# Opening order of the loads: three pieces of the input projection first, A_log and the attention constants behind the convolutions

## The chip, the cores and the metric

The kernel runs on one core of a Trainium2 chip. The metric is device time in microseconds (us) of one launch, from which the median of several runs is taken. A core has a matrix engine (TensorE, in the views PE, and PEld for its weight loads), VectorE (DVE), ScalarE (ACT), GpSimd (POOL) and SyncE (SP). In this kernel SP does nothing but issue DMAs; its rows in the timeline, marked SPq, show the time that each issue took on the queue, not the transfer. [...]

## What is computed

The reference is one decoder layer on x of shape (8, 512, 512) in float32, with a layer norm after each of three parts:

```
x = layernorm(x + mamba(x))                 # ln, in_proj, causal conv (4 taps), silu, x_proj, dt, scan, gate, out_proj
x = layernorm(x + cross_attention(x, ctx))  # 16 heads of 32
x = layernorm(x + mixture_of_experts(x))    # 32 experts, 4 for each token, plus a shared one
```

The change touches the start of the first part. There, for each sequence, `xz = xn @ in_proj_w` gives x_main and z (1024 columns each), x_main goes through a convolution of four taps along time and a silu, `x_dbl = x_main @ x_proj_w` gives dt, B and C, and the scan is `h = exp(A dt) * h + dt B x`, with `A = -exp(A_log)` of shape (1024, 16).

## The kernel before

**Chunks.** The function `layers` cuts the 8 sequences of 512 steps into 16 chunks of 256 steps. Inside a chunk 32 steps run over four pairs of channel blocks (q), four groups of states (g) and the two blocks of a pair: `decays` (L437, ACT) makes exp(A dt), `scan` multiplies (L449) and scans (L453) on DVE, and `collect` multiplies by C (L470, DVE) and sums over states on PE (L474). Attention and routing of the sequence before are placed between the steps. The function `experts` runs the 32 experts after that, and `finish` the last layer norm.

**The start.** Ahead of the first step stand: the load of the first chunk of x (L168), its layer norm (L74 to L80), the transposes (L286) and their scaling by ln_w and ln_b (L291), four convolutions, `silu` (L353), `x_proj` (L359) with its result stored to DRAM (L367), `prepare` (dt and dt x, L389 to L412) with the copies `both` (L418), and the broadcasts `bc` (L378) of B and C. A convolution (`convolve`) is a projection on PE (L302, 16 matmuls with one piece of in_proj_w), a copy out of PSUM on ACT (L322), the first tap on ACT (L328) and six instructions for the other taps on DVE (L336). Buffer `xp`, which L322 writes, is there once, so a convolution's copy waits for the taps of the one before.

**The pieces of weights.** `pieces()` is a generator over the 512 KB pieces of in_proj_w and out_proj_w in the order of their use; three buffers named `wm` hold them. Each piece is loaded by SP (L156). `begun` draws the first piece at once. The generator loads one piece ahead of the one that it hands out: the start loads pieces 0 and 1, the second convolution asks for piece 2 while it takes piece 1, the third asks for piece 3, the fourth for piece 4, which is the first of z.

**The constants.** After `begun(pieces())` the source loads nine small constants with `const` (L131: ln_w to res_scale), then A_log in 16 DMAs of 4 KB (L185, into `aneg`), then bq, bk, bv, bo and wg (L131). Further down, behind memsets on POOL, six DMAs (L241) put rows of ones into the three attention buffers `ka`, and one DMA writes zeros to the DRAM tensor `based` (L258). The first use of `aneg` is an exponential on ACT (L1032) and a negation on DVE (L1033); both are in place, ahead of the first `decays`. bq, bv and bo are used in `biases` (L974, L986, L990), which also takes the attention mask (L976 to L980).

**What sets the order.** The source order is a wish. The tile framework's planner puts the instructions of each engine in an order of its own, by the source order as a priority and by its own estimate of when inputs and buffers are there; only `silu` is pinned. That is why in the trace before the weights Wo (L525), the mask (L976) and the next chunk of x (L271), which stand inside the first chunk's steps in the source, are issued at 29 to 31 us, and why some of the 32 DMAs that fill the experts' input buffer with zeros (`clear`, L262, 1362.5 KB each), also placed inside the first two chunks, are issued before the first scan. Within `layers` the calls stand in this order:

```
    for q in range(CC // 2):
        do(convolve, 0, q, f, first=(q == 0))
    dry()
    silu(*f["xs"].values())
    do(x_proj, f)
    dry()
    do(prepare, 0, f)
    dry()
    bc, n = bcast(f, 0), 0
```

Of the kernel before, what the change touches and what calls it, by code (L numbers as in the profile page):

```python
# [8 lines left out]
F32 = mybir.dt.float32  # L9
# [8 lines left out]
P = 128  # L18
B, S, D = 8, 512, 512
DC = D // P  # L20
# [4 lines left out]
NST = 16  # L25
# [4 lines left out]
NG = 4  # L30
HP = P // 2
NPB = 3

NH = 16
HD = 32
SC = S // P

E = 32
# [44 lines left out]
def layers(ctx, tc, a, x1d, filld, based, xbuf):  # L83
# [23 lines left out]
    nc = tc.nc  # L107
# [3 lines left out]
    cp = ctx.enter_context(tc.tile_pool(name="l_const", bufs=1))  # L111
# [17 lines left out]
    def const(name, shape, src):  # L129
        t = cp.tile(shape, F32, name=f"l_{name}")  # L130
        nc.sync.dma_start(t, src)  # L131
        return t

    def rows(w):
        return w.rearrange("(c p) f -> p c f", p=P)

    def pieces():


        w_in, w_out = rows(a["in_proj_w"]), rows(a["out_proj_w"])  # L140
        xs = [w_in[:, :, 2 * q * P : 2 * (q + 1) * P] for q in range(CC // 2)]
        zs = [w_in[:, :, DI + 2 * q * P : DI + 2 * (q + 1) * P] for q in range(CC // 2)]
        outs = [w_out[:, 2 * q : 2 * q + 2, :] for q in range(CC // 2)]
        n = B * (S // T)
        order = list(xs)
        for i in range(n):
            order += (outs if i else []) + zs + (xs if i + 1 < n else [])
        order += outs
        got = None
        for src in order + [None]:  # L150
            nxt = None
            if src is not None:
                nxt = mp.tile([P, 4 * 2 * P], F32, tag="wm", name="wm", bufs=3).rearrange(
                    "p (c f) -> p c f", c=src.shape[1]
                )
                nc.sync.dma_start(nxt, src)  # L156
            if got is not None:
                yield got
            got = nxt

    def begun(it):
        first = next(it)
# [4 lines left out]
    x0 = p1.tile([P, NT_, D], F32, tag="xt", name="xt")  # L167
    nc.sync.dma_start(x0, a["x"][0, 0:T, :].rearrange("(j p) d -> p j d", p=P))  # L168
    piece = begun(pieces())
    lnw = const("lnw", [P, DC], a["ln_w"])  # L170
    lnb = const("lnb", [P, DC], a["ln_b"])
# [4 lines left out]
    b_dt = const("b_dt", [P, CC], a["dt_proj_b"])  # L176
    dpar = const("dpar", [P, CC], a["D_param"])
    rs = const("rs", [P, 1], a["res_scale"].partition_broadcast(P))

    aneg = cp.tile([P, CC, 2, NST // NG, NG // 2], F32, name="l_aneg")  # L180
    for r in range(2):
        for j in range(2):
            for g in range(NST // NG):
                n0 = g * NG + r * NG // 2
                nc.sync.dma_start(  # L185
                    aneg[r * HP : (r + 1) * HP, :, j, g, :],
                    rows(a["A_log"])[j * HP : (j + 1) * HP, :, n0 : n0 + NG // 2],
                )
    bq = const("bq", [P, DC], a["bq"])
    bk = const("bk", [P, DC], a["bk"])  # L190
    bv = const("bv", [P, DC], a["bv"].rearrange("(c p) -> p c", p=P))
    bo = const("bo", [P, D], a["bo"].partition_broadcast(P))
    wg = const("wg", [P, DC, E], rows(a["wg"]))

    conv_tail = cp.tile([P, CC, 3], F32, name="l_conv_tail")
# [8 lines left out]
    ones = cp.tile([P, P], F32, name="l_ones")  # L206
# [26 lines left out]
    qas, kas = [], []  # L233
    for i in range(NPB):
        qas.append(cp.tile([P, S], F32, name=f"l_qa{i}"))
        kas.append(cp.tile([P, S], F32, name=f"l_ka{i}"))
        for t in (qas[i], kas[i]):
            for r0 in (HD, 2 * HD + HD):
                nc.gpsimd.memset(t[r0 : r0 + HD], 1.0 if t is qas[i] else 0.0)
        for r0 in (HD + 1, 2 * HD + HD + 1):  # L240
            nc.sync.dma_start(  # L241
                kas[i][r0 : r0 + 1, :].rearrange("p (c t) -> p c t", c=DC),
                ones[0:1, :].unsqueeze(1).to_broadcast([1, DC, P]),
            )
    va = cp.tile([P, SC, NH // 2, 3 * HD], F32, name="l_va")
    nc.gpsimd.memset(va[:, :, :, HD : 2 * HD], 1.0)

# [12 lines left out]
    def clear(e):  # L260

        nc.sync.dma_start(  # L262
            xbuf[e * CAP : (e + 1) * CAP, :].rearrange("(j p) d -> p j d", p=P),
            zero.unsqueeze(1).to_broadcast([P, CJ, ROW]),
        )

# [81 lines left out]
    def silu(*tiles):  # L350

        for v in tiles:
            tc.keep_in_program_order(nc.scalar.activation(v, v, AF.Silu))  # L353
        tc.keep_in_program_order(nc.scalar.preload_act_table_set(LN_EXP))
# [16 lines left out]
    def bcast(f, g):  # L371

        got = []
        for r0 in (g * NG, NST + g * NG):
            t = bcp.tile([P, NG // 2, T], F32, tag="bc", name="bc")
            for r in range(2):
                n0 = r0 + r * NG // 2
                nc.sync.dma_start(  # L378
                    t[r * HP : (r + 1) * HP], f["scr"][n0 : n0 + NG // 2, :].partition_broadcast(HP)
                )  # L380
            got.append(t.unsqueeze(1).to_broadcast([P, 2, NG // 2, T]))
        return got
# [613 lines left out]
    def settle():  # L996

        got = [part() for part in left]
        left[:] = [x for x in got if x]

    def dry():
        while left:
            settle()

    def do(fn, *args, first=False):

        if first:
            dry()
        rest = fn(*args)
        settle()  # L1010
        if rest:
            left.append(rest)
# [10 lines left out]
    for q in range(CC // 2):  # L1023
        do(convolve, 0, q, f, first=(q == 0))
    dry()
    silu(*f["xs"].values())
    do(x_proj, f)
    dry()
# [2 lines left out]
    bc, n = bcast(f, 0), 0  # L1031
# [5 lines left out]
    for i, (b, t) in enumerate(chunks):  # L1037
# [8 lines left out]
        for k, (q, g, ci) in enumerate(steps):  # L1046
# [61 lines left out]
            while i < 2 and cleared < E * (i * len(steps) + k - 6) // (2 * len(steps) - 7):  # L1108
                clear(cleared)
                cleared += 1  # L1110
        while t and side:
            _, fn, alone = side.pop(0)
# [310 lines left out]
def program(tc, a, out):  # L1423
    nc = tc.nc
    with tc.tile_pool(name="dram", bufs=1, space=DRAM) as dram:
        x1d = dram.tile([N, D], F32, name="x1d")
        filld = dram.tile([B, S], F32, name="filld")

        based = dram.tile([N + P, D], F32, name="based")
        xbuf = dram.tile([SLOTS, ROW], F32, name="xbuf")  # L1430
        nc.scalar.preload_act_table_set(LN_EXP)

        with ExitStack() as ctx:
            layers(ctx, tc, a, x1d, filld, based, xbuf)
        with ExitStack() as ctx:
            experts(ctx, tc, a, xbuf, based)
        with ExitStack() as ctx:
            finish(ctx, tc, based, out)
# [31 lines left out]
```

## Time and profile before

| | |
|---|---|
| median of 3 runs | 5567.89 us (5564.01 to 5571.6) |
| the profiled execution's own time | 5569.36 us |
| its span, first to last instruction | 5567.7 us |
| mean granted TensorE clock | 0.937 |
| PE busy | 4880.6 us (88%) |
| DVE busy | 4349.5 us (78%) |
| ACT busy | 2592.1 us (47%) |
| POOL busy | 569.2 us (10%) |
| DMA, mean over the span | 138 GB/s |

Times in the views are counted from the start of the span. In the chunks, up to about 3600 us, DVE is busy 213 to 220 us of every 240; in the experts' stage, from about 3950 us, PE is the busy engine. In the first 70 us no engine is: there PE is busy 44.2 us, ACT 28.3 us and DVE 20.6 us, and the first scan's multiplication (L449) starts at 69.93 us. The share of busy time over the whole span says nothing on those 70 us; they have to be read from the timeline.

### The profile page before, as it was taken

The numbers are of one execution on the slowest core, as the hardware profiler recorded it, in microseconds if no ns is written. First come the engines' busy times: TensorE is split into PE (matmuls) and PEld (weight loads), VectorE is DVE, ScalarE is ACT, GpSimd is POOL, SyncE is SP. The second block draws the span as 40 slices with busy tenths as digits, with TensorE's granted clock in tenths as the row PEclk, the third lists the DMA queues.
The fourth block names the chain that finished last, engine by engine and source line by source line (L and its number), as shares of the span: only waits on it lengthen the run. The fifth ranks groups of instructions, "written<-read, shape, count | busy, mean of one in ns | idle before, by whom it ended". The sixth has DMA issues, their size and how long they took to land. (4 is left out here: it accounts for less than half of the span.)

```text
span 5567.7 us, 60361 instructions
## 1 busy us (share of the span) xinstructions
PE 4880.6 (88%) x19752; PEld 2718.5 (49%) x19752; DVE 4349.5 (78%) x5738; ACT 2592.1 (47%) x5481; POOL 569.2 (10%) x424
## 2 busy tenths in 40 slices
PE   6668889888888988888898898879899999999994
PEld 4334344334434434443443443333577777777773
DVE  6998899989889999898989999864466565555554
ACT  4555555655566455555555656523222222222223
POOL 1000002001100200200020020010111111111111
PEclk8778999999999999999999999989999999999997
DMA  6787355444634634643463454441345454544444
GB/s 187 226 229 211 109 137 176 121 118 143 178 106 112 201 97 129 184 124 108 122 207 98 120 188 113 112 158 45 96 125 126 124 126 119 126 125 120 119 121 145
DMA packets 554282, 769.83 MB, mean 138 GB/s; under 512 B 135754, under 2 KB 268394, under 8 KB 551920
## 3 DMA queue, kind: packets, MB, share of 16 engines
q1 hardware_dynamic: 517952, 677.55, 41.6%
q0 software_dynamic: 33280, 76.90, 7.4%
q10 hardware_dynamic: 2736, 11.54, 0.5%
q8 instruction: 156, 2.56, 0.2%
q14 instruction: 158, 1.29, 0.1%
HBM read 508.68 MB, written 165.05 MB: 121 GB/s over the span
## 5 line engine op out<-in xcount | busy, mean ns | idle before, releaser
L437 ACT ACTIVATE l_da<-both,l_aneg 128x256 f32<-128x256 f32 x2048 | 888.4, 499 | 790.6 <-DVE h L453 745.9
L453 DVE TENSOR_TENSOR_SCAN h<-l_da,h 128x1028 f32<-128x1028 f32 x512 | 1170.0, 2292 | 50.7 <-ACT h L443 27.3
L474 PE MATMUL py<-h,l_twice 128*64 128x256 f32 x4096 | 627.5, 421 | 195.1 <-DVE h L470 194.9
L449 DVE TENSOR_TENSOR h<-both,bc 128x1024 f32<-128x1024 f32 x512 | 617.9, 1214 | 142.5 <-PE py L474 81.6
L470 DVE TENSOR_TENSOR h<-h,bc 128x1024 f32<-128x1024 f32 x512 | 622.6, 1219 | 6.3 <-DMA l_ka<-filld 0.3
L474 PEld LDWEIGHTS py<-h,l_twice 128*64 128x64 f32 x4096 | 292.5, 147 | 568.8 <-issue 237.7
L1220 PE MATMUL ps_h<-xT,w 128*128 128x320 f32 x1536 | 435.6, 433 | 0.0
L766 PE MATMUL ps_s<-l_ka,l_qa 64*128 64x512 f32 x1024 | 314.1, 692 | 137.4 <-DVE mx L768 137.2
L1300 POOL DMA_INDIRECT based<-y,xe x160 | 252.1, 1576 | 1313.5 <-ACT y L1323 571.3
L1241 DVE TENSOR_TENSOR hT<-ps_h,p 128x320 f32<-128x320 f32 x128 | 62.9, 492 | 379.0 <-PE ps_h L1220 379.0
L768 DVE TENSOR_REDUCE mx<-ps_s 128x2 f32<-128x1024 f32 x256 | 310.4, 1216 | 55.4 <-PE ps_s L766 54.7
L1220 PEld LDWEIGHTS ps_h<-xT,w 128*128 128x128 f32 x1536 | 292.2, 190 | 118.2 <-issue 0.4
L792 PE MATMUL ps_t<-l_qa,l_ka 64*128 64x512 f32 x1024 | 299.6, 648 | 20.9 <-ACT eT L796 17.5
L796 ACT ACTIVATE eT<-ps_t 128x1024 f32<-128x1024 f32 x256 | 259.1, 1013 | 110.1 <-PE ps_t L792 109.6
L808 PE MATMUL po<-eT,l_va 128*64 128x512 f32 x1024 | 281.4, 629 | 24.5 <-ACT raw L820 20.8
L641 POOL DMA_INDIRECT xbuf<-x2t,dest x128 | 218.8, 1709 | 814.6 <-DVE dest L635 776.2
L1220 PE MATMUL ps_h<-t,s 128*128 128x320 f32 x1024 | 286.1, 432 | 0.0
L302 PE MATMUL ps_z<-xnT,wm 128*128 128x256 f32 x1024 | 240.9, 389 | 17.4 <-DVE o L512 16.4
L302 PE MATMUL ps_x<-xnT,wm 128*128 128x256 f32 x1024 | 245.6, 394 | 11.1 <-DMA wm<-in_in_proj_w 10.1
L703 PE MATMUL ps_p<-x2T,wa 128*128 128x512 f32 x512 | 243.9, 625 | 11.8 <-DVE hT L883 10.3
L503 PE MATMUL po<-wm,zs 128*128 128x512 f32 x512 | 236.9, 613 | 9.8 <-DVE k L688 5.3
L1220 PEld LDWEIGHTS ps_h<-t,s 128*128 128x128 f32 x1024 | 194.6, 190 | 81.1
(234 smaller groups left out, 7422.5 us busy)
## 6 DMA issues: line engine op xcount, KB each, us to landing
bc<-scr SPq DMA_DIRECT2D x1024, 128.0 KB
w<-in_w SPq DMA_DIRECT2D x93, 1024.0 KB
wm<-in_in_proj_w SPq DMA_DIRECT2D x128, 512.0 KB
xbuf<-zero SPq DMA_DIRECT2D x32, 1362.5 KB
xe<-xbuf SPq DMA_DIRECT2D x32, 1362.5 KB
both<-dt SPq DMA_DIRECT2D x256, 128.0 KB
both<-dtx SPq DMA_DIRECT2D x256, 128.0 KB
wm<-in_out_proj_w SPq DMA_DIRECT2D x64, 512.0 KB
```

What stands on the lines that cost most here:

```text
L302: nc.tensor.matmul(ps[:, i, :], w[:, dc, i * P : (i + 1) * P], f["xnT"][:, dc, :], start=(dc == 0), stop=(dc == DC - 1),)
L437: nc.scalar.activation(da[:, n, 1:], dt[:, c % 2, j, :], AF.Exp, scale=aneg[:, c, j, g, m : m + 1])
L449: nc.vector.tensor_tensor(steps, dtx[:, c % 2].unsqueeze(2).to_broadcast([P, 2, NG // 2, T]), bc[0], ALU.mult)
L453: nc.vector.tensor_tensor_scan(flat, da.rearrange("p n t -> p (n t)"), flat, 0.0, ALU.mult, ALU.add)
L470: nc.vector.tensor_tensor(steps, steps, bc[1], ALU.mult)
L474: nc.tensor.matmul(py[j * HP : (j + 1) * HP, c % 2, :], twice, h[:, j * 2 + m, 1:], start=False, stop=(s == (NST // NG - 1, NG // 2 - 1, 1)),)
L766: nc.tensor.matmul(ps[:, j, :], qa[r, lt * P : (lt + 1) * P], ka[r, :], start=True, stop=True)
L768: return lambda: nc.vector.tensor_reduce(mx[:, lt, :].unsqueeze(2), ps, AX.X, ALU.max) and None
L792: nc.tensor.matmul(ps[:, j, :], ka[r, kc * P : (kc + 1) * P], qa[r, :], start=True, stop=True)
L796: nc.scalar.activation(eT, ps, AF.Exp)
L808: nc.tensor.matmul(po[j * 2 * HD : (j + 1) * 2 * HD, :], va[:, kc, i, j * HD : (j + 2) * HD], eT[:, j, :], start=(kc == 0), stop=(kc == SC ...
L1220: nc.tensor.matmul(ps, w[:, n, r * P : (r + 1) * P], x[:, n, :], start=not more and n == 0, stop=n == 1, skip_group_check=more,)
```

## The change

Three things are moved, and nothing is computed differently.

`pieces()` now loads three pieces before it hands out the first. It then hands out the second without a load, and from the third on it goes as before: one load, one piece handed out. So the third piece's load stands third on SP's list in the source, ahead of ln_w; the loads of pieces 3 and 4 stay with the third and the fourth convolution.

The 16 loads of A_log, the six loads of rows of ones and the loads of bq, bk, bv, bo and wg are moved into a function `later_constants`, called after the `dry()` that ends the four convolutions and before `silu`. Their tiles are allocated where they were. The memsets on POOL stay where they were.

```diff
@@ pieces()
-        got = None
-        for src in order + [None]:
+        got = []
+        for n, src in enumerate(order + [None]):
             nxt = None
             if src is not None:
                 nxt = mp.tile([P, 4 * 2 * P], F32, tag="wm", name="wm", bufs=3).rearrange(
                     "p (c f) -> p c f", c=src.shape[1]
                 )
                 nc.sync.dma_start(nxt, src)
-            if got is not None:
-                yield got
-            got = nxt
+            got.append(nxt)
+
+            for _ in range((0, 0, 2, 1)[min(n, 3)]):
+                yield got.pop(0)
@@ layers(), after res_scale
+    bq = cp.tile([P, DC], F32, name="l_bq")
...
-    for r in range(2):
-        for j in range(2):
-            for g in range(NST // NG):
-                n0 = g * NG + r * NG // 2
-                nc.sync.dma_start(
-                    aneg[r * HP : (r + 1) * HP, :, j, g, :],
-                    rows(a["A_log"])[j * HP : (j + 1) * HP, :, n0 : n0 + NG // 2],
-                )
-    bq = const("bq", [P, DC], a["bq"])
-    bk = const("bk", [P, DC], a["bk"])
-    bv = const("bv", [P, DC], a["bv"].rearrange("(c p) -> p c", p=P))
-    bo = const("bo", [P, D], a["bo"].partition_broadcast(P))
-    wg = const("wg", [P, DC, E], rows(a["wg"]))
@@ the loop over kas
-        for r0 in (HD + 1, 2 * HD + HD + 1):
-            nc.sync.dma_start(
-                kas[i][r0 : r0 + 1, :].rearrange("p (c t) -> p c t", c=DC),
-                ones[0:1, :].unsqueeze(1).to_broadcast([1, DC, P]),
-            )
@@ behind clear()
+    def later_constants():
+        for r in range(2):
+            for j in range(2):
+                for g in range(NST // NG):
+                    n0 = g * NG + r * NG // 2
+                    nc.sync.dma_start(
+                        aneg[r * HP : (r + 1) * HP, :, j, g, :],
+                        rows(a["A_log"])[j * HP : (j + 1) * HP, :, n0 : n0 + NG // 2],
+                    )
+        for i in range(NPB):
+            for r0 in (HD + 1, 2 * HD + HD + 1):
+                nc.sync.dma_start(
+                    kas[i][r0 : r0 + 1, :].rearrange("p (c t) -> p c t", c=DC),
+                    ones[0:1, :].unsqueeze(1).to_broadcast([1, DC, P]),
+                )
+        nc.sync.dma_start(bq, a["bq"])
+        nc.sync.dma_start(bk, a["bk"])
+        nc.sync.dma_start(bv, a["bv"].rearrange("(c p) -> p c", p=P))
+        nc.sync.dma_start(bo, a["bo"].partition_broadcast(P))
+        nc.sync.dma_start(wg, rows(a["wg"]))
@@ after the four convolutions
     dry()
+    later_constants()
     silu(*f["xs"].values())
```

More of the change, by code (lines that the diff above doesn't have):

```diff
@@ L178, in layers @@
     rs = const("rs", [P, 1], a["res_scale"].partition_broadcast(P))
-    aneg = cp.tile([P, CC, 2, NST // NG, NG // 2], F32, name="l_aneg")
-    for r in range(2):
-        for j in range(2):
-            for g in range(NST // NG):
-                n0 = g * NG + r * NG // 2
-                nc.sync.dma_start(
-                    aneg[r * HP : (r + 1) * HP, :, j, g, :],
-                    rows(a["A_log"])[j * HP : (j + 1) * HP, :, n0 : n0 + NG // 2],
-                )
-    bq = const("bq", [P, DC], a["bq"])
-    bk = const("bk", [P, DC], a["bk"])
-    bv = const("bv", [P, DC], a["bv"].rearrange("(c p) -> p c", p=P))
-    bo = const("bo", [P, D], a["bo"].partition_broadcast(P))
-    wg = const("wg", [P, DC, E], rows(a["wg"]))
+    bq = cp.tile([P, DC], F32, name="l_bq")
+    bk = cp.tile([P, DC], F32, name="l_bk")
+    bv = cp.tile([P, DC], F32, name="l_bv")
+    bo = cp.tile([P, D], F32, name="l_bo")
+    wg = cp.tile([P, DC, E], F32, name="l_wg")
+    aneg = cp.tile([P, CC, 2, NST // NG, NG // 2], F32, name="l_aneg")
     conv_tail = cp.tile([P, CC, 3], F32, name="l_conv_tail")
```

## The prediction, made before the changed kernel was seen

> **What bounds the kernel now.** I read the page first: DVE is the busiest engine of the chunks and PE of the experts. The change touches neither stage, only the start, so the view that counts is the waits between 10 and 72 us. In it each line names who waited, for whom, the sum, how often, and the longest.
>
> ```profile
> DVE fl L978 <- DMA mu<-in_mask: 11.0, 1, 11.0
> PE ps_x L302 <- DMA wm<-in_in_proj_w: 10.1, 1, 10.1
> DVE h L449 <- DMA bc<-scr: 9.1, 1, 9.1
> ```
>
> The middle line is one single wait of PE for a piece of weights. Why the piece was late is seen in the timeline of SP's issues (start, length of the group, what, how many):
>
> ```profile
> 1.31 1.00 SPq L156 DMA_DIRECT2D wm<-in_in_proj_w  x2
> ...
> 9.31 10.91 SPq L185 DMA_DIRECT2D l_aneg<-in_A_log  x16
> ...
> 22.99 4.13 SPq L241 DMA_DIRECT2D l_ka<-l_ones  x6
> 27.21 0.39 SPq L258 DMA_DIRECT2D based<-zero  x1
> 27.66 1.57 SPq L156 DMA_DIRECT2D wm<-in_in_proj_w  x3
> ```
>
> Piece 2 is the first of the group at 27.66. Ahead of it SP spent 10.91 us on A_log, 22.86 - 20.27 = 2.6 us on five constants and 4.13 us on the rows of ones, though it never had to wait. The timeline of PE and ACT shows what this costs:
>
> ```profile
> 12.14 9.43 PE L302 MATMUL ps_x<-xnT,wm 128*128 128x256 f32 x32 [0.26 <-ACT xnT L291]
> ...
> 31.65 9.90 PE L302 MATMUL ps_x<-xnT,wm 128*128 128x256 f32 x32 [10.08 <-DMA wm<-in_in_proj_w]
> ...
> 42.25 0.59 ACT L322 COPY xp<-ps_x 128x512 f32<-128x512 f32 x1 [2.21 <-DVE xs L336]
> ```
>
> Convolutions 0 and 1 end on PE at 21.57; convolutions 2 and 3 start at 31.65. Last, the windows cut at these points say whether other work could take the gap's place:
>
> ```profile
> 12.00:21.60 9.60, 9.43 (x32) 7.62 (x32) 2.11 (x5) 2.67 (x6) 0.19 (x1) 1.00 0.38 6
> 21.60:31.60 10.00, 0.00 (x0) 0.00 (x0) 3.40 (x10) 1.88 (x4) 0.41 (x3) 0.77 0.52 146
> 31.60:41.60 10.00, 9.90 (x32) 7.97 (x32) 2.43 (x6) 1.68 (x3) 0.19 (x1) 0.72 0.87 289
> 41.60:70.00 28.40, 22.69 (x82) 14.70 (x83) 9.74 (x29) 17.47 (x34) 0.80 (x2) 0.88 0.92 271
> ```
>
> After the stretch come busy times of PE, PEld, DVE, ACT and POOL, the granted clock, the DMA share and GB/s. In the gap all engines are nearly idle and DMA moved 6 GB/s before it: SP's issue time was the bound, not the transfers. From 70 to 250 us DVE shows hardly an idle microsecond (20.00 of 20 in most windows), so a scan that starts earlier ends earlier.
>
> **What the Trainium skill says.** "TensorE: Matmul & The Clock Gate", Part 1: PE's clock halves after an idle window of about 3.4 us and returns after a busy one. The trace agrees: finer windows show the clock at 0.50 from 28 to 36 us, after the gap, and again from 46 to 50, after a pause from 41.55 to 46.18. The same page, under the engine queue depths, calls ACT and DVE strict FIFO; here L978 stood at the head of DVE for 11.0 us. "DMA: Bandwidth & Descriptors", "HWDGE ordering": on an engine descriptors are consumed in ring order, so a transfer queues behind earlier ones. The trace fits: the mask, 4 KB, was issued at 29.84 behind 2.6 MB and released L978 at 37.56.
>
> **Part by part.** The sum is made against the profiled execution: span 5567.7, own time 5569.36, which is 1.5 above the median of 5567.89; I take the difference off the median.
>
> *Piece 2 loaded third.* Its issue leaves 27.66 for about 2.3. One load took 27.66 to its first use at 31.65, 4.0 us; even behind 1.5 MB at the 376 GB/s that the DMA view shows (4 us) it is there by 11, and is wanted at 21.57. The wait of 10.1 goes. What is late next? PE itself: 4.7 us for each convolution, so 21.57, 26.3, 31.0. DVE's six taps take 2.7 and a convolution's chain on ACT and DVE (copy 0.59, first taps, taps) about 4.1, shorter than PE's 4.7. The copy of convolution 3 then starts at 31.05 instead of 42.25, and its first tap at 31.7 instead of 43.09 (0.26 of which was a wait for POOL): **11.4 us**, 1.3 more than the wait, because the clock stays at 1.0 and no copy waits for taps.
>
> *What is pushed back by piece 2.* Nine constants issue 0.5 us later (1.57/3), and 512 KB stand before ln_w: 1.4 us at 376 GB/s. ln_w is wanted by L291 at 11.06; three 512 KB transfers end by about 7.5 by the rates of the DMA view, so it lands about 8 to 9 now and 9.5 to 10.5 then. Cost 0 to 1, taken 0.3.
>
> *The 27 moved DMAs.* Their 17.5 us of issue (gaps counted) stay on SP. If SP finds them behind the fourth convolution's load, which waits for convolution 1 (21.57), they run to about 39.5; if the planner lifts them into SP's idle time, from 10 to 28. scr (L367), wanted next, is issued at 52.58 - 11.4 = 41.2: hidden both ways, by at least 1.7 us. Behind them in SP's list stand Wo, the mask, the next x and zeros. Piece 3's load needs convolution 0's buffer (free at 16.9) and is used at 26.3; planned in the midst of the constants it lands by 21 to 29: cost 0 to 2.7, taken 0. First uses: aneg at 66.82 less the gain, but L1032 and L1033 stand earlier, and bq at L974. Should they be planned ahead of taps and land late they hold up ACT or DVE: 0 to 3, taken 0.5. bv and bo are used at 42 and 58, the rows of ones after 500 us. POOL's list is untouched; only the ones' DMAs wait for its memsets, done by 9.3.
>
> *x_proj.* It ran 5.97 us at half clock, where 16 projection matmuls at full clock ran 3.72. Its pause shrinks from 4.6 to 3.75 us (31.0 to 34.75), about the window of the clock. The gain is 0 to 2.2; taken 1.1.
>
> *The rest of the start.* dt is ready 11.4 earlier, then eight copies and four broadcasts issued by SP, 60.12 to 68.4, set the first L449 at 69.93. Unchanged. DMA moved 3.1 MB between 28 and 38; about 8 MB, with four fills of zeros, went out before 60 at up to 390 GB/s, that is 22 us. Compressed by 11 this would end near 50, about when dt's copies go out (48.7): 0 to 3, taken 0, as the planner should place fewer fills in a shorter gap.
>
> Sum: -11.4 + 0.3 + 0.5 - 1.1 = **-11.7**, so 5567.89 - 11.7 = **5556.2**. The tell-apart bound of 0.2% is 11.1 us: the forecast lies only just beyond it.
>
> **The rivals.**
>
> *The gap's fillings move into the scan.* During the gap DVE did work of later places for nothing: L974, L978, L979, L986 (0.16 + 0.41 + 0.41 + 0.61) and the norm of the next chunk (2.65 from 42.93 to 50.42). If the constants now stand before Wo, mask and next x in SP's list, and these behind scr and the broadcasts, that 4.2 us lands where DVE is full. Then -11.7 + 4.2 = -7.5: 5560.4. For it: the source order gives the constants priority over all of these. Against: SP has 13 us to spare before scr if it issues as fast as here.
>
> *The gain stops at the next piece.* All constants stand before piece 3; it is issued at 27.5 and lands at 31.5, and convolution 3 waits 5 us. -11.7 + 5.2 = -6.5: 5561.4. So the change would do only half of what it says. Against it: in the list of before the planner put pieces 3 and 4 ahead of Wo as soon as it reached them.
>
> *Slower: the zeros.* Four fills of 1362.5 KB went out in the old start. If none does, 5.45 MB more have to pass in the chunks up to 480 us, where the DMA share is already 0.85 (240 to 480 us) and DVE once waited 8.1 us for a z gate behind late pieces. At 300 GB/s that is 18 us. It decides once more than 11.7 us of it show up as DVE waits, and with the 4.2 of fillings all of it gives -11.7 + 4.2 + 18 = +10.5, with a further wait for a piece about +12: 5580. Against it: by the end of chunk 0 the fills stood on their source positions, so the early ones were only early. A reshuffled order further on, of either sign, I put at some 4 us.
>
> **How the numbers follow.** Forecast 0.58 (faster 0.44, within 0.13, slower 0.01), fillings 0.24 (0.02 faster, 0.22 within), next piece 0.05 (within), zeros 0.13 (0.12 slower, 0.01 within). So faster 0.46, within 0.41, slower 0.13. The forecast's bounds are 11.4 + 2.2 + 4 = 17.6 faster (5550) and, all losses in and the clock's gain out, 11.4 - 9.7 = 2 faster (5566); taking in the low rivals and part of the zeros gives 5550 to 5573.
>
> **What would show it.** In the changed profile: the 10.1 us wait gone, L302 of all four convolutions in one run from about 12 to 31; first silu table load near 33; scr at 39 to 41; the first L449 at 57 to 59. Next: whether L74 of the next chunk and L986 stand before that L449 (forecast) or after it (fillings); how many fills come before it (4 now). The forecast is wrong if PE waits for `wm` again, if L291 waits for DMA, if DVE or ACT stand at L978, L1032 or L1033, or if the first L449 comes by 11 us earlier and the end does not.

## The result: 8.9 us less, and the profile after

The changed kernel has a median of 5553.9 us over 20 runs (5546.48 to 5563.21); the kernel before, run beside it on the same chip, 5562.81 us over 20 runs (5550.64 to 5571.6). The ratio is 0.9984, with an interval from 0.9977 to 0.9991: 8.9 us less, with 5.0 to 12.8 us as the bounds. The forecast was 11.7 less. The profiled execution of the changed kernel has a span of 5554.1 us (its own time 5555.79), 13.6 below that of before; so this pair of profiles shows more than the medians do, by less than the scatter of the runs. Each profile is one execution, and every figure of a timeline below is that of one.

The diff moves the line numbers: L302 is now L311, L322 is L331, L336 is L345, L353 is L362, L359 is L368, L367 is L376, L378 is L387, L418 is L427, L449 is L458, L474 is L483, L486 is L495, L978 is L987, L990 is L999, A_log's L185 is L260. In the experiments they differ again by a few, so I name the tiles.

The timeline of the start (start in us, length of the group, engine or queue, line, tiles, how many; in brackets the idle time before, and what ended it):

```profile
1.31 1.55 SPq L156 DMA_DIRECT2D wm<-in_in_proj_w  x3
...
10.77 2.09 SPq L260 DMA_DIRECT2D l_aneg<-in_A_log  x3
12.13 15.34 PE L311 MATMUL ps_x<-xnT,wm 128*128 128x256 f32 x64 [0.26 <-ACT xnT L300]
...
17.14 0.39 SPq L156 DMA_DIRECT2D wm<-in_in_proj_w  x1
...
21.02 7.42 SPq L260 DMA_DIRECT2D l_aneg<-in_A_log  x11
...
29.55 0.59 ACT L331 COPY xp<-ps_x 128x512 f32<-128x512 f32 x1 [2.37 <-DVE xs L345]
...
33.31 6.26 PE L368 MATMUL ps_d<-xs,l_w_x 128*64 128x256 f32 x16 [5.84 <-ACT xs L362]
...
40.00 0.34 SPq L376 DMA_DIRECT2D scr<-xd  x1
...
41.49 3.54 SPq L387 DMA_DIRECT2D bc<-scr  x5
46.85 2.65 SPq L427 DMA_DIRECT2D both<-dt  x4
49.60 2.55 SPq L427 DMA_DIRECT2D both<-dtx  x4
...
54.33 2.36 DVE L458 TENSOR_TENSOR h<-both,bc 128x1024 f32<-128x1024 f32 x2 [4.11 <-DMA both<-dtx]
```

The same places in the kernel before:

```profile
18.16 0.59 ACT L322 COPY xp<-ps_x 128x512 f32<-128x512 f32 x1 [5.16 <-PE ps_x L302]
...
60.12 2.72 SPq L418 DMA_DIRECT2D both<-dt  x4
...
65.98 8.82 SPq L378 DMA_DIRECT2D bc<-scr  x14
...
69.93 2.36 DVE L449 TENSOR_TENSOR h<-both,bc 128x1024 f32<-128x1024 f32 x2 [9.14 <-DMA bc<-scr]
```

All 64 matmuls of the four convolutions now stand in one run, where before there were two runs of 32 with 10.08 us between them. Piece 3 (17.14) is issued as soon as convolution 0 has given its buffer back, ahead of most of A_log. The last copy is held by the taps of the convolution before it (2.37 from L345), as it was (2.21), but no copy waits for a late piece any more. Every later event is earlier by more than the 10.1 us wait: the copy of convolution 3 by 12.7, scr by 12.6, the copies of dt by 13.3, the first L458 by 15.6. About 1.0 of each is scatter and not the change's: the first convolution's copy comes 6.0 us after PE's start in the profile of before and 5.0 in this one, and over all profiles, those of the experiments too, it comes after 4.6 to 6.0 us, on both sides of the change (5.2 with the pieces alone, 6.0 with the constants alone).

The waits of all engines between 10 and 57 us, the lines that answer to the three of before:

```profile
PE ps_d L368 <- ACT xs L362: 5.8, 1, 5.8
...
DVE fl L987 <- DMA mu<-in_mask: 5.1, 1, 5.1
...
DVE h L458 <- DMA both<-dtx: 4.1, 1, 4.1
```

The wait of `ps_x` for `wm` is not in the list. The mask still holds L987, for 5.1 us instead of 11.0, and the first multiplication now waits last for a copy of dt x and not for `bc`. PE's longest wait is that for the silus.

Windows of the changed kernel (us, busy time of PE, PEld, DVE, ACT, POOL, granted clock, DMA share, GB/s):

```profile
17.10:27.50 10.40, 10.37 (x49) 8.78 (x47) 6.03 (x14) 5.03 (x9) 0.77 (x5) 1.00 0.56 105
27.50:33.30 5.80, 0.00 (x0) 0.00 (x0) 4.27 (x11) 3.63 (x6) 0.29 (x2) 0.87 0.18 5
33.30:39.60 6.30, 6.26 (x16) 3.29 (x16) 0.67 (x3) 3.11 (x5) 0.00 (x0) 0.58 0.65 180
```

The second line is PE's pause ahead of x_proj, 5.8 us where it was 4.6: PE ends its convolutions early and waits for ACT and DVE. The third shows the price, a clock of 0.58 over x_proj.

What became of the lead can be read at the starts of the chunks, that is at scans 1, 33, 65 and so on in the trace:

| us | first scan | scan 33 | scan 65 | last scan | end |
|---|---|---|---|---|---|
| before | 72.2 | 240.8 | 433.4 | 3688.8 | 5567.7 |
| after | 56.6 | 232.8 | 421.8 | 3680.6 | 5554.1 |
| difference | -15.6 | -8.0 | -11.7 | -8.2 | -13.6 |

Half the lead is lost in the first chunk, and a part comes back in the second. From scan 1 to 33 DVE of before took 168.6 us (167.1 of work, 1.6 idle); after, 176.2 (169.8 and 6.4). What the idle time was, DVE's waits from 54 to 235 us say:

```profile
DVE h L458 <- DMA both<-dtx: 4.1, 1, 4.1
DVE h L458 <- DMA bc<-scr: 2.9, 1, 2.9
DVE zs L495 <- PE py L483: 2.0, 1, 2.0
DVE xs L345 <- ACT xs L337: 1.5, 1, 1.5
```

The first line lies before the first scan. The other three make 6.4; before, the same chunk had 1.6 (1.4 of it for py). The 2.7 us of work are mostly the layer norm of the next chunk, which in the kernel before ran ahead of the first scan, from 42.93 to 50.42, and is now among DVE's groups of this stretch (busy us, mean ns, idle), with its first line:

```profile
L74 DVE BATCH_NORM_STATS2 st<-xt 128x6 f32<-128x512 f32 x2 | 1.3, 672 | 0.0
```

Over two chunks the loss is 365.1 - 361.2 = 3.9 us: 2.0 of work and 1.9 of idle time. What is left, 15.6 - 3.9 = 11.7, lies inside the interval of the measurement. The differences between -8 and -14 further on are of the size by which the runs scatter; I draw nothing from them.

### The profile page after: what moved, and what is told of

Read it like the earlier page. It is cut to its first block, busy times and chain, and to the rows that moved or that the text cites. A ratio compares the mean times of both kernels' runs of the same rounds, so it can differ in the third digit from the quotient of the medians.

```text
span 5554.1 us, 60352 instructions
## 1 busy us (share of the span) xinstructions
PE 4883.9 (88%) x19752; PEld 2720.5 (49%) x19752; DVE 4349.2 (78%) x5738; ACT 2592.8 (47%) x5483; POOL 560.9 (10%) x424
## 5 line engine op out<-in xcount | busy, mean ns | idle before, releaser
L483 PE MATMUL py<-h,l_twice 128*64 128x256 f32 x4096 | 632.0, 424 | 194.2 <-DVE h L479 194.0
L458 DVE TENSOR_TENSOR h<-both,bc 128x1024 f32<-128x1024 f32 x512 | 617.5, 1213 | 141.8 <-PE py L483 78.2
L483 PEld LDWEIGHTS py<-h,l_twice 128*64 128x64 f32 x4096 | 295.2, 148 | 570.5 <-issue 246.4
L311 PE MATMUL ps_z<-xnT,wm 128*128 128x256 f32 x1024 | 241.0, 389 | 17.8 <-DVE o L521 17.0
L311 PE MATMUL ps_x<-xnT,wm 128*128 128x256 f32 x1024 | 242.5, 390 | 2.9 <-DMA wm<-in_in_proj_w 2.0
```

The source lines that it names most:

```text
L311: nc.tensor.matmul(ps[:, i, :], w[:, dc, i * P : (i + 1) * P], f["xnT"][:, dc, :], start=(dc == 0), stop=(dc == DC - 1),)
L458: nc.vector.tensor_tensor(steps, dtx[:, c % 2].unsqueeze(2).to_broadcast([P, 2, NG // 2, T]), bc[0], ALU.mult)
L483: nc.tensor.matmul(py[j * HP : (j + 1) * HP, c % 2, :], twice, h[:, j * 2 + m, 1:], start=False, stop=(s == (NST // NG - 1, NG // 2 - 1, 1)),)
```

## The experiments

Each is compared with the kernel before on the same chip; differences in us are the ratio's distance from 1 times 5562. The theory: SP's issue time was the bound, the constants' new place gives the lead, and the first chunk takes some of it back. Rivals: the pieces alone do it; the clock or the zeros decide; the transfers and not their issue were late.

**Pieces alone.** Before, with only the hunk of `pieces()`; the constants stay in front.

```diff
-        got = None
-        for src in order + [None]:
+        got = []
+        for n, src in enumerate(order + [None]):
...
+            for _ in range((0, 0, 2, 1)[min(n, 3)]):
+                yield got.pop(0)
```

> The kernel before with the three pieces loaded first, A_log and the other constants left in front. Theory (the bound of the start is SP's issue time ahead of the next piece, so each part of the change is worth what it takes off the piece that is wanted next): convolution 2 no longer waits, but piece 3 is still issued behind 27 constants at about 28 us and lands near 31.5, so PE waits some 5 to 8 us for it ahead of convolution 3; the copy of convolution 3 comes near 36 (42.25 before, 29.55 in the changed kernel), the first multiplication of the scan near 63 to 65 (69.93 and 54.33), and the time is 4 to 6 us below before. Rival (loading three pieces first is what matters, the place of the constants not): all of the 15.6 us at the first multiplication, and a time some 9 us below before.

Measured: 5566.16 us, ratio 1.0005 (0.9999 to 1.0012), no gain where 4 to 6 us were expected. Its timeline:

```profile
28.97 1.00 SPq L156 DMA_DIRECT2D wm<-in_in_proj_w  x2
...
33.08 6.31 PE L303 MATMUL ps_x<-xnT,wm 128*128 128x256 f32 x16 [9.44 <-DMA wm<-in_in_proj_w]
...
67.10 2.36 DVE L450 TENSOR_TENSOR h<-both,bc 128x1024 f32<-128x1024 f32 x2 [8.88 <-DMA bc<-scr]
```

The wait moved on by one piece: piece 3 leaves at 28.97 behind the constants, and convolution 3 waits 9.4 us for it where convolution 2 had waited 10.1. The prediction's rival of the next piece describes what happens in this kernel, though it put the wait at 5 us; it needs the constants in front.

**Constants alone.** After, with the old `pieces()` that loads one ahead.

```diff
-        got = []
-        for n, src in enumerate(order + [None]):
+        got = None
+        for src in order + [None]:
...
```

> The changed kernel with the loading of pieces as before (one ahead); only the constants stand behind the convolutions. Theory (SP's issue time): the planner can now issue piece 2 right behind the nine small constants at about 10 us, it lands by 15, before PE wants it at 21, so nothing is lost: first multiplication of the scan within 1 us of 54.3, time within 2 us of the changed kernel, some 9 us below before. Rival (the early third piece is what matters): PE waits for a piece again, the first multiplication comes 4 or more us later than 54.3.

Measured: 5554.74 us, ratio 0.9985 (0.9979 to 0.9992), the same as the whole change. In its timeline

```profile
9.11 0.43 SPq L156 DMA_DIRECT2D wm<-in_in_proj_w  x1
9.59 1.42 SPq L259 DMA_DIRECT2D l_aneg<-in_A_log  x2
...
34.25 5.05 PE L367 MATMUL ps_d<-xs,l_w_x 128*64 128x256 f32 x16 [5.84 <-ACT xs L361]
...
54.11 2.36 DVE L457 TENSOR_TENSOR h<-both,bc 128x1024 f32<-128x1024 f32 x2 [1.09 <-DMA both<-dtx]
```

piece 2 goes out at 9.11, right behind the nine small constants, early enough for its use near 20, and the first multiplication starts 0.2 before that of the change. So the gain is that of the constants' place; loading three pieces at once adds nothing that these runs can tell. x_proj took 5.05 us here and 6.26 in the change, after the same pause of 5.84.

**A_log twice, before.** Before, with each of A_log's 16 DMAs issued a second time into a tile that nobody reads.

```diff
                 nc.sync.dma_start(aneg[...], rows(a["A_log"])[...])
+                nc.sync.dma_start(again[...], rows(a["A_log"])[...])
```

> The kernel before with each of the 16 loads of A_log doubled into a tile that nobody reads. Theory (SP's issue time ahead of piece 2 is the bound, the bytes are not): SP issues piece 2 some 10.9 us later, at 38.5, PE's wait grows from 10.1 to about 21, and the first multiplication comes at about 80.8 instead of 69.93; time up by 8 to 11 us. Rival (the wait for the piece is hidden by something else, or ended by the transfers): the first multiplication moves by less than 4 us.

Measured: 5573.15 us, ratio 1.0019 (1.001 to 1.0027), 10.6 slower.

```profile
9.70 0.75 SPq L186 DMA_DIRECT2D l_aneg<-in_A_log  x1
10.49 0.62 SPq L190 DMA_DIRECT2D l_again<-in_A_log  x1
...
38.88 1.57 SPq L156 DMA_DIRECT2D wm<-in_in_proj_w  x3
...
42.84 8.88 PE L307 MATMUL ps_x<-xnT,wm 128*128 128x256 f32 x32 [21.54 <-DMA wm<-in_in_proj_w]
```

Sixteen more DMAs of 4 KB, 64 KB in all, move piece 2's issue by 38.88 - 27.66 = 11.2 us and PE's wait by 11.5. Each of the added ones holds SP for 0.63 us, 0.68 with the gap to the next, with hardly a byte to carry: the issue time is the bound. Nor did piece 2 find a backlog of transfers in the kernel before: from 26 to 28 us, just ahead of its issue, the DMA share was 0.01. The first scan came 9.2 later; in this profile the two convolutions behind the wait ran 8.88 us, not 9.90, and x_proj 5.35, not 5.97.

**A_log twice, after.** The same edit where the loads are now.

```diff
             for g in range(NST // NG):
                 nc.sync.dma_start(aneg[...], rows(a["A_log"])[...])
+                nc.sync.dma_start(again[...], rows(a["A_log"])[...])
```

> The changed kernel with each of the 16 loads of A_log doubled into a tile that nobody reads. Theory: the pieces keep their places, the convolutions end as in the changed kernel; SP had 4.6 us to spare between the last constant (34.9, Wo's issue behind it 35.4) and scr (40.0), so of the 10.9 us about 6 show at scr and at the first multiplication (about 60); time up by 3 to 6 us against the changed kernel. Rival (constants behind the convolutions are hidden whatever they take): the first multiplication stays at 54 to 55.

Measured: 5568.08 us, ratio 1.0007 (0.9999 to 1.0016); against the change some 13 slower.

```profile
12.13 16.06 PE L316 MATMUL ps_x<-xnT,wm 128*128 128x256 f32 x64 [0.26 <-ACT xnT L305]
...
47.65 0.44 SPq L381 DMA_DIRECT2D scr<-xd  x1
```

The convolutions don't feel the added DMAs, as the pieces keep their places; scr does, at 47.65 instead of 40.00. In the changed kernel SP issues its last constant at 34.39 and Wo behind it to 35.4, so it has 4.6 us to spare before scr; 11 more overrun that. I expected the first scan about 6 later; it came 8.5 later, and the first chunk took 180.7 us. SP's overrun at scr is not the whole way: A_log's exponential stood on ACT until 42.34, behind the later loads and ahead of the copy that makes xd, so PE waited 2.3 us for xd (0.46 in the change) and dt's copies went out 3.4 later; and the five broadcasts that the change issues ahead of dt's copies now stood behind all eight, from 59.03. In the change the moved DMAs were free because SP's room was large enough for them, and not for many more.

**The next x early.** After, with the load of the second chunk's x ahead of the late constants, so that its norm falls into the convolutions again.

```diff
+    nf0 = {}
+    load_x(*chunks[1], nf0)
     later_constants()
...
-        nf = {}
+        nf = {} if i else nf0
...
-                if k == 5:
+                if k == 5 and i:
```

> The changed kernel with the load of the second chunk of x placed ahead of the moved constants. Theory (of the 15.6 us won at the first scan, part is given back in chunk 0 because the norm of the next chunk, 2.6 us of DVE, has moved out of the idle start into the scans): the norm goes back in front of the first scan, chunk 0 (first scan to 33rd scan) shortens from 176.2 to about 173.5 us (168.6 before), the first multiplication stays within 1 us of 54.3, and the time is 2 to 3 us below the changed kernel. Rival (the give-back is waits alone, on the broadcasts behind zeros and on PE): chunk 0 stays at 175 to 177 us.

Measured: 5553.1 us, ratio 0.9983 (0.9976 to 0.9989); from the change that can't be told.

```profile
19.84 0.69 DVE L74 BATCH_NORM_STATS2 st<-xt 128x6 f32<-128x512 f32 x1
...
55.38 2.36 DVE L458 TENSOR_TENSOR h<-both,bc 128x1024 f32<-128x1024 f32 x2 [2.04 <-DMA both<-dtx]
```

The norm did go into the convolutions (19.84), and DVE's work in the first chunk fell from 169.8 to 168.2. Its idle time stayed at 6.5, and the start came 1.0 later. So the moved norm explains 1.6 us of the first chunk's loss; whether taking it back is worth anything in time, these runs can't tell.

**Four fills of zeros early.** After, with the four first fills issued ahead of the first scan, as before had them.

```diff
     later_constants()
+    for e in range(4):
+        clear(e)
...
-    old, side, cleared = None, [], 0
+    old, side, cleared = None, [], 4
```

> The changed kernel with four of the 32 fills with zeros put back into the start, behind the moved constants. Theory (the fills that left the start cost little later): their 5.45 MB stand ahead of scr and dt's copies in the DMA rings, so the first multiplication comes 1 to 4 us later than 54.3; chunks 0 and 1 shorten by what the broadcasts waited behind fills, 1 to 3 us; sum 0, time within 3 us of the changed kernel. Rival (the displaced fills ate the difference between the 15.6 us won at the first scan and the 9 us won at the end): chunks 0 and 1 together shorten by 5 us or more and the time falls by 4 us or more below the changed kernel.

Measured: 5566.77 us, ratio 1.0009 (1.0001 to 1.0018).

```profile
35.23 5.68 SPq L249 DMA_DIRECT2D xbuf<-zero  x4
...
59.86 2.36 DVE L458 TENSOR_TENSOR h<-both,bc 128x1024 f32<-128x1024 f32 x2 [11.85 <-DMA bc<-scr]
```

The first multiplication waits 11.85 us for `bc`, behind the zeros, and the two first chunks get no shorter for having four fills less (373.2 us, 365.1 in the change). So putting them back is worse as a whole. It isn't a clean test of whether the displaced zeros hold up the chunks: Wo and the mask were pushed behind the first scan as well (60.92 and 64.04), DVE's work in the two chunks grew by 2.4 us, and while the wait of 2.9 for `bc` in the first chunk went, one of 4.8 for a copy of dt x came.

**The clock kept up.** After, with ten matmuls that no one uses ahead of the silus, so that PE isn't idle before x_proj.

```diff
     later_constants()
+    keep = pss.tile([P, 2, S], F32, tag="sc", name="keep")
+    for _ in range(10):
+        nc.tensor.matmul(keep[:, 0, :], ident, f["xs"][1].rearrange("p i t -> p (i t)"), start=True, stop=True)
```

> The changed kernel with ten more matmuls of 512 columns, of no use to the result, on PE between the fourth convolution and x_proj. Theory (x_proj runs at half clock because PE pauses for 5.8 us ahead of it): the granted clock stays at 1.0 from 27 to 38 us, x_proj takes 3.7 to 4.2 us instead of 6.26, and xd, scr and the first multiplication come about 2.3 us earlier; time 2 to 3 us below the changed kernel. Rival (x_proj's matmuls are bound by something else, its weights being 64 columns wide): x_proj stays near 6 us although the clock is up.

Measured: 5557.68 us, ratio 0.9989 (0.9982 to 0.9996), some 3 less gain than the change has, with intervals that overlap.

```profile
26.38 8.75 PE L1038 MATMUL keep<-xs,l_ident 128*128 128x512 f32 x20
...
32.36 1.28 ACT L1045 ACT_TABLE_LOAD   x1
...
35.05 3.71 PE L368 MATMUL ps_d<-xs,l_w_x 128*64 128x256 f32 x16
...
57.97 2.36 DVE L458 TENSOR_TENSOR h<-both,bc 128x1024 f32<-128x1024 f32 x2 [3.23 <-DMA both<-dtx]
```

x_proj took 3.71 us instead of 6.26, at a clock of 1.00 from 24 to 44 us: against the change's profile the half clock cost 2.5 us. But the ten ran to 35.13 and x_proj started 1.7 late; the planner put A_log's exponential between two silus, with two more table loads of 1.28 us on ACT; and dt's chain on DVE stood behind the addition for bo. The first multiplication came 3.6 later. This run shows the clock, not what it is worth, so it was done again with five matmuls and the exponential held in its place.

```diff
+    for _ in range(5):
+        nc.tensor.matmul(keep[:, 0, :], ident, f["xs"][1].rearrange("p i t -> p (i t)"), start=True, stop=True)
...
-    nc.scalar.activation(aneg, aneg, AF.Exp)
+    tc.keep_in_program_order(nc.scalar.activation(aneg, aneg, AF.Exp))
```

> The changed kernel with five instead of ten idle matmuls between the fourth convolution and x_proj, and the exponential of A_log kept in its place behind the silus. Theory (the half clock costs x_proj 2.5 us; the first try lost it again because the idle matmuls ran past the silu and other work was planned into dt's chain): x_proj takes about 3.7 us and starts no later than in the changed kernel, scr is issued at about 37.5 (40.0), the first multiplication comes at about 52 (54.3), the time is 1 to 3 us below the changed kernel. Rival: something else sets the first multiplication (the mask ahead of dt in DVE's list, the broadcasts behind dt's copies on SP), which stays at 54 or later.

Measured: 5562.93 us against 5562.88 of before, ratio 0.9996 (0.9987 to 1.0004). The start did what was expected:

```profile
33.13 3.67 PE L368 MATMUL ps_d<-xs,l_w_x 128*64 128x256 f32 x16 [1.55 <-ACT xs L362]
...
37.23 0.34 SPq L376 DMA_DIRECT2D scr<-xd  x1
...
52.18 2.35 DVE L458 TENSOR_TENSOR h<-both,bc 128x1024 f32<-128x1024 f32 x2
```

It is the earliest first multiplication of all, 2.2 us ahead of the change, and the time can't be told from that of the kernel before. DVE's waits from 52 to 235 us:

```profile
DVE zs L495 <- PE py L483: 6.9, 2, 4.9
DVE l_bo L999 <- PE ps_bo L996: 5.0, 1, 5.0
DVE h L458 <- DMA bc<-scr: 3.2, 1, 3.2
```

In the first chunk the idle time went from 6.4 to 10.2 us, 4.9 of it in one wait of a gate for `py`; its 32 scans took 179.9. The 5.0 of L999 lie just ahead of the first multiplication, which followed it without a wait of its own. Of the lead of 17.8 at the first scan 6.4 was left at the 33rd; how much of that is due to the five matmuls and how much to the exponential's place was not separated. The interval of this run and that of the change overlap, so a loss against the change is not shown.

**Copies of dt x on ACT's queue.** After, with SP's eight copies before the first multiplication shared out: dt on SP, dt x on ACT. "DMA: Bandwidth & Descriptors" of the Trainium skill, "Issuing engines are not separate DMA queues", says that issuing on several engines saves only the sequencer's time and that the transfers share the same DMA engines. SP's 2.55 us for the second four (49.60) are such time.

```diff
+    f["first"] = True
     do(prepare, 0, f)
     dry()
+    f["first"] = False
...
-                            nc.sync.dma_start(to[...], src[...])
+                            start = nc.scalar.dma_start if src is dtx and f.get("first") else nc.sync.dma_start
+                            start(to[...], src[...])
```

That is its second form. In the first the flag, `"late" not in f`, was never set for later chunks, so 244 of the 256 copies of dt x went to ACT:

> The changed kernel, with the four copies of dt x of the first pair of channels issued from ACT's queue and not from SP's. In the changed kernel SP issues eight copies one behind the other (46.85 to about 52), and the first multiplication, at 54.33, waited last for a copy of dt x. If SP's issue time sets the first scan, the copies of dt x go out some 2 us earlier, the first multiplication starts at 52 to 53, the broadcasts behind them come up to 2.6 us earlier and the wait of 2.9 us for bc in the first chunk shrinks: 3 to 5 us faster than the changed kernel. If the transfers, not their issue, set it, the start stays at 54.3 and the time with it. A third outcome: the start gains and the first chunk gives it back, as when the clock was kept up: 32 scans in over 178 us and no gain in time.

> The same with the load of the second chunk's x put ahead of the late constants too, so that its norm falls into the convolutions and not into the first chunk. If the two work independently, the first scan starts as in the run with the copies on ACT, up to 1 us later, and the first 32 scans take about 2 us less than there: 3 to 7 us faster than the changed kernel, at about 5547 to 5551 where the changed one has 5554. If what the first chunk wins is given back by the third or fourth chunk, as in the run with the next x early alone, it is within 2 us of the changed kernel.

Measured: 5633.39 us, ratio 1.0131 (1.0114 to 1.0148), and with the next x early 5637.32, ratio 1.0143 (1.0126 to 1.016). The first two chunks show nothing of it: scan 65 came 9.3 us before that of the kernel before, the last scan 57.5 after it. The growth comes in the chunks behind, where ACT issues the copies among the exponentials; that ACT's time for issuing is the cause is likely and was not shown. Then with the four alone:

> The run before with copies on ACT issued 244 of the 256 copies of dt x from ACT's queue, those of all later chunks as well, and grew by 4 to 5 us with each chunk; here only the four of the first pair of channels of the first chunk are on ACT. Theory A, the transfers and not SP's issue set the first multiplication: it starts as there, at about 55.8 (54.33 in the changed kernel), the first 32 scans take about 176, and with the later copies back on SP the time comes back to 5552 to 5558, no faster than the changed kernel. Theory B, the four copies of the first pair alone gain and the later ones hid it: 3 to 5 us faster than the changed kernel, 5549 to 5551. If the growth came from the start and not from the 240 later copies, the time stays at about 5630.

Measured: 5556.38 us, ratio 0.9995 (0.9986 to 1.0003), its theory A. The timeline of that kernel:

```profile
47.70 3.46 SPq L428 DMA_DIRECT2D both<-dt  x4
48.39 3.06 ACTq L428 DMA_DIRECT2D both<-dtx  x4
...
55.71 2.36 DVE L459 TENSOR_TENSOR h<-both,bc 128x1024 f32<-128x1024 f32 x2 [4.37 <-DMA both<-dtx]
```

The last copy is issued by 51.45, not 5.30 us but 3.75 after the first, yet the multiplication follows the first copy by 8.0 us where it was 7.5 with SP alone. The page holds here: sharing out saved issue time and no time of landing. From 50 to 54 us the DMA share was 0.98 and 1.12: at this place the transfers are the bound; at A_log's it was the issue. SP's next broadcasts went out from 51.21, not 52.20, and so ran beside the last copies; how much they took from them was not separated.

**All runs side by side**, each profile's scans against those of before, and the measured time (in us, from the ratio):

| | scan 1 | scan 65 | measured |
|---|---|---|---|
| the change | -15.6 | -11.7 | -8.9 |
| constants alone | -15.8 | -7.0 | -8.3 |
| next x early | -14.5 | -9.8 | -9.5 |
| ten idle matmuls | -12.0 | -6.6 | -6.1 |
| five idle matmuls | -17.8 | -8.1 | -2.2 |
| four copies on ACT | -14.2 | -7.8 | -2.8 |
| pieces alone | -2.8 | -1.7 | +2.8 |
| four zeros early | -10.1 | +1.9 | +5.0 |
| A_log twice, after | -7.1 | +3.4 | +3.9 |
| A_log twice, before | +9.2 | +9.6 | +10.6 |

The measured figures are good to 4 to 5 us, those of the scans are of one execution each. The start of the third chunk stands within 6 us of each; the first scan misses by 11 to 16 in four of them. Every kernel that starts its scans earlier loses some of it in the first two chunks, from 1.1 us (pieces alone) to 12.0 (zeros early); the one that starts later loses 0.4 more. No version beats the change by more than its interval.

## Why the prediction was right, and the terms that were not

The direction, the mechanism of the start and the range held: 8.9 less against 11.7. That 5553.9 stands so near the forecast 5556.2 is in part luck: the kernel before has 5562.81 over 20 runs and not the 5567.89 of three, from which the forecast was taken off. The likeliest case put just more than the 0.2% bound, the measurement just less; of the three chances "faster by over 0.2%" had the most and "within 0.2%" came. The forecast's sum is at the same time what the trace shows at scan 65, but partly by errors that cancel.

*Piece 2.* The wait of 10.1 went whole, and SP's issues ahead of piece 2 were the cause, as the doubled A_log shows; that piece 2 is now loaded third was not needed for it. The term that was mis-sized is PE's 4.7 us for a convolution: four take 15.34, that is 3.8 each. The 4.7 was half of 9.43, a run that begins with the slow first convolution (its copy starts at 18.16, 6.0 us after PE's start). So the chain on ACT and DVE sets the pace, with copies at 21.27 and 25.41, 4.14 apart, the 4.1 that the text had worked out and set aside as shorter. The fourth copy came at 29.55, not 31.05: 1.5 more gained. Only 0.5 of that is the pace: from 18.16 on, three steps of 4.14 lead to 30.6. The other 1.0 is the first convolution, which happened to be shorter in this profile.

*ln_w and the waits in order.* The 0.3 and 0.5 cost nothing: L311 starts at 12.13 (12.14 before), and scr and dt came ahead of their forecasts although DVE stood 5.1 us at L987 and 2.2 at L1043 (L1033 of before). The prediction had named such waits as signs of a wrong forecast; they came and were harmless.

*The moved DMAs.* They went out from 10.77 to 34.82, between the prediction's two cases (10 to 28, and until 39.5), ahead of scr as it said. Their issue adds up to 17.8 us by the lines of before, not 17.5; nothing hung on that.

*x_proj.* The step failed. It took a gain of 1.1 from a pause of 3.75; PE ended 3.5 earlier than forecast and the silus only 1.4, so the pause grew to 5.8 us and x_proj ran 6.26 us, 0.3 longer than before. The pause was the wrong number, but the forecast pause of 3.75 would hardly have given the gain either: with the pieces alone one of 3.93 was followed by 6.27 us. With the pause filled x_proj took 3.7. The 0.3 itself says little, as x_proj took 5.05 to 6.63 us in the six profiles with a pause of 5.8.

*The rest of the start.* "Unchanged" was wrong by 3.0. Between scr and dt's first copy 0.7 went; between that copy and the first multiplication 2.3 (7.48 us instead of 9.81). Five broadcasts are now issued at 41.49, ahead of dt's copies, where before all 14 stood behind them, and the first multiplication no longer waits last for one.

Together: -11.7 - 1.5 + 1.4 - 0.8 - 3.0 = -15.6, which is the first scan.

*After the first scan* the sum had no term: the forecast took it that a scan that starts earlier ends earlier, as DVE hardly idled in the first chunk. That step failed. An earlier start found waits that DVE didn't have before, and the sign that the prediction had named, a first multiplication earlier by 11 us and an end that isn't, came in part: 15.6 at the start, 8.9 (5.0 to 12.8) at the end. There the rival of the fillings came true in part: the norm of the next chunk moved into the first chunk, 1.6 us by the run with the next x early; the biases and the mask's arithmetic stayed in front. To it came waits for `bc` (2.9), for convolution taps (1.5) and for `py` (0.6 more than before). Over two chunks that makes 3.9 back, to -11.7.

*The rivals.* The next piece didn't come, because the planner takes piece 3's load at the moment its buffer is free; with the constants in front it does. The zeros' case had its premise, as none stands before the first scan, but not its size: it put up to 18 us of DVE waits into the chunks, and over the first two DVE's idle time grew by 1.9. Whether the fills caused the wait for `bc` among them was not separated.

What stays open is why the lead lost in the first chunk differs so much between versions. It goes into waits for `bc`, for `py` and for copies of dt, in an order that the planner makes anew for each kernel; which of them an earlier start must make longer was not separated.

## What to carry to other kernels

When a transfer is late, look first at what its queue issued ahead of it and how long each issue took: 27 DMAs of constants, sixteen of them of 4 KB, cost PE 10 us here, and moving them was the gain, while loading the wanted piece earlier without moving them only passed the wait to the next piece. Before moving issues behind a point, compare their sum with the queue's idle time there: 4.6 us were left here, and 11 more us overran them. Read the worth of a faster start not at the first instruction of the bound engine but some chunks on, after the first waits behind it: 15.6 us at the first scan were 8.9 at the end.

## What the runs showed of the hardware

A start at half clock costs x_proj's 16 matmuls 1.4 to 3.0 us: 5.05 to 6.63 us after a pause of 5.8 us (6.26 in the change, at a mean clock of 0.58; 5.05 with the constants alone, at 0.72), and 3.67 after one of 1.55, at a clock of 1.00. "TensorE: Matmul & The Clock Gate" of the Trainium skill, Part 1, has the window of about 3.4 us; the two pauses lie on either side of it. I had not expected that ending PE's work earlier would leave what follows as slow as it was. Nor that a load of 4 KB, cut as A_log is, holds SP for 0.63 us (median of the 16), longer than the 0.38 to 0.53 us of 512 KB of weights. And the same four 128 KB copies on a second queue land no sooner, while 244 of them on ACT's queue, in place of SP's, cost 1.3% of the time.
